# Two attention layers on one core: where the second layer's values, the projections and the next image's transposes stand in the order of work

## The chip, the core and the metric

The kernel runs on one core of a Trainium2 chip. The metric is device microseconds for one execution, the median of repeated runs; lower is better. Engines are named as in the profile: PE is TensorE (PEld its weight loads), DVE is VectorE, ACT ScalarE, POOL GpSimd, SP SyncE. Each has its own queue, and semaphores join them.

## The reference

Eight images of 32 x 32 positions (N = 1024 rows) and C = 256 channels, all float32, pass through two attention layers:

```python
# layer 0: four heads of width C
qkv = xf @ W_qkv                                  # b n (h, 3C)
atten = softmax((q @ k.T) * C ** -0.5)            # per head, over the keys
res = concat_h(atten @ v) @ W_out + b_out
x = res + xf
# layer 1: one head with keys of width 32
f, g, h = x @ Wf + bf, x @ Wg + bg, x @ Wh + bh
o = softmax(g @ f.T) @ h
y = gamma * o + x
```

## The kernel before

**Work and steps.** Weights are folded first (`fold_weights`: query with key weights, value with output weights), so that layer 0 is, for each head and each block of 512 queries: scores (`Layer0.scores`, L558), exponentials, a product of the probabilities with the image (`products`, L655), and a projection with the folded value weights (`project`, L676). All of these go by `seven` (L235), a seven-product scheme for 2 x 2 blocks of matrices: it has three tasks, `one`, `two` and `three`. Each puts matmuls on PE and then the reads of their banks on ACT and DVE. The operands of its seven products are sums of blocks, made by DVE: `query_sums` of q, `key_sums` of the image (L421, tile `xs`), `sums` of the probabilities (L593, tile `ss`, four pieces of 1024 columns), and the `ysums` of `project` (tile `yt`).

The list `steps` (L956) has one entry for each unit (a head, or layer 1 of the image before) and each of its two blocks. Images 1 to 6 run head 0, head 1, layer 1 of the image before, head 2, head 3; the last image has layer 1 of image 6 after its four heads, and layer 1 of image 7 follows behind all steps. In the text, "the third head" is head 2.

**The order.** PE, DVE and ACT carry out exactly the order in which tasks are called. In each step of the loop at L982, `put(tasks, *at)` notes a place between 0 and 10 for each task; at the end of the step the tasks are called in the order of these places, and of their `put` where places are equal. SP and POOL, which issue the DMAs, are ordered by the scheduler. A step scores its own block, makes sums and product tasks `one` and `two` of the step before (`one` at L984), and product task `three`, the reciprocal (`invert`, L637) and the projection of the step before that (`two`).

**Names that the change touches.**

- Layer 1's first step (`blk == 0`): `values` (L786) has five tasks. The first sets a column of ones on POOL; each of the other four has eight matmul passes (`pr_v_l`) and one DVE read into `v_l` (L794). Also here: `scores` of layer 1 (`ps_l`, L811), the product of head 1's second block (`psx_y`, `psy_y`, `psz_y`), the projection of its first block (`psx_o`, `psy_o`), and `turned1`, four DVE transposes (L394) of the image behind.
- Banks: `seven` takes three of the six `ps` banks for scores and products. For a projection (`two_banks`) it takes both `psm` banks, one for `x`, one for `y` and `z`. Values, too, take a `psm` bank each.
- `adds` (L697): DVE multiplies the projected tile `o` by the reciprocals `invb` (L699); POOL then adds `o` to `x1T` by an accumulating DMA (L702). The tile `o` has one buffer, so the next projection's first writes to `o` (ACT's copy of the `x` bank, L284, and DVE) wait until that DMA has landed.
- `invert` makes four reciprocals per row on DVE (L641); SP writes them to DRAM (`inv`, L646) and reads them back as a row for all partitions (`invb`, L648).
- The next image's transposed copy: `turn_rows` (L401) gives 8 `moves`, each with four SP DMAs (L386, `x0T`), and `turned`, four DVE transposes of 32 x 32 squares (L394). `key_sums` come from the result. They stand around the third head.
- Before the first step: matmuls of a zero tile (L947) while the first weights load, then transposes and products of weights (L312, L327, L365).

Of the kernel before, what the change touches and what calls it, by code (L numbers as in the profile page):

```python
# [20 lines left out]
def kernel(  # L21
# [89 lines left out]
    def tile_of(tag, shape, name):  # L111
        return pools[tag].tile(shape, F32, tag=tag, name=name)
# [4 lines left out]
    def load_x(b, parts=1):  # L117
        t = tile_of("rows", [P, NT, C], f"x_{b}")
        n = HT // parts
        for k in range(NBLK):  # L120
            for i in range(parts):
                nc.sync.dma_start(
                    t[:, k * HT + i * n : k * HT + (i + 1) * n, :].rearrange("p t c -> p (t c)"),
                    x_v[b][:, k, ts(i, n * C)],
                )
        rows[b] = t
# [78 lines left out]
    def sum_a(sums, a11, a12, a21, a22):  # L205
        tt = nc.vector.tensor_tensor
        s1, s2, s3, s4 = sums
        return [
            partial(tt, s1, a21, a22, ALU.add),
            partial(tt, s2, s1, a11, ALU.subtract),  # L210
            partial(tt, s3, a11, a21, ALU.subtract),
            partial(tt, s4, a12, s2, ALU.subtract),
        ]
# [11 lines left out]
    def a_operands(blocks, sums):  # L225
        a11, a12, a21, a22 = blocks
        s1, s2, s3, s4 = sums
        return dict(zip((1, 2, 3, 4, 5, 6, 7), (a11, a12, s4, a22, s1, s2, s3)))
# [172 lines left out]
    def turn_rows(b):  # L401


        def end():
            if b not in xT_of:
                xT_of[b] = tile_of("xT", [P, CC, N], f"x0T_{b}")
            return xT_of[b].rearrange("p c (n i) -> p c n i", i=P)

        return squares(end, lambda: rows[b].rearrange("p n (c i) -> p n c i", i=P), False)
# [11 lines left out]
    def key_sums(b):  # L421

        made = {}

        def piece(i):
            if i == 0:
                xT = xT_of[b]
                t = tile_of("v", [P, 4, HN], f"xs_{b}")
                sums = [t[:, k, :] for k in range(4)]
                blocks = [xT[:, c, ts(k, HN)] for k in range(2) for c in range(CC)]  # L430
                made["l"] = sum_a(sums, *blocks)
                xblocks[b] = a_operands(blocks, sums)
            made["l"][i]()

        return [partial(piece, i) for i in range(4)]

    def value_sums(b):

        made = {}

        def piece(i):
            if i == 0:
                r = rows[b]
                t = tile_of("xt", [P, 4, NT // 2, P], f"xt_{b}")
                blocks = [r[:, ts(j, NT // 2), ts(c, P)] for j in range(2) for c in range(CC)]
                sums = [t[:, k] for k in range(4)]
                made["l"] = sum_b(sums, *blocks)
                vblocks[b] = b_operands(blocks, sums)
            made["l"][i]()

        return [partial(piece, i) for i in range(4)]

    def residual(b):


        def piece(c):
            if c == 0:
                x1T_of[b] = tile_of("xT", [P, CC, N], f"x1T_{b}")
            nc.scalar.activation(
                x1T_of[b][:, c, :], xT_of[b][:, c, :], AF.Identity, bias=boutT_sb[:, c : c + 1]  # L460
            )

        return [partial(piece, c) for c in range(CC)]
# [479 lines left out]
    nc.vector.memset(idle, 0.0)  # L943
    ident = identity()
    pm = tile_of("psm", [P, NB], "pm_idle")
    for _ in range(5):
        nc.tensor.matmul(pm[:, :P], lhsT=idle, rhs=idle, start=True, stop=True)  # L947
    for h, tag in ((1, "rows"), (2, "v"), (3, "xT")):
        run(load_weights(h, tag))
# [6 lines left out]
    steps, adds = [], {}  # L956
# [16 lines left out]
    def is_l0(s):  # L973
        return s is not None and isinstance(s[0], Layer0)

    def step(k):
        return steps[k] if 0 <= k < len(steps) else None
# [4 lines left out]
    for i, (a, blk) in enumerate(steps):  # L982
        l0 = isinstance(a, Layer0)
        one, two, nxt = step(i - 1), step(i - 2), step(i + 1)  # L984
        places = []

        def put(tasks, *at):
            assert len(tasks) == len(at)
            places.extend(zip(at, range(len(places), len(places) + len(at)), tasks))

        if l0:
            put(a.scores(blk), 0, 2, 4, 6, 8, 10)
        else:
            tasks, _ = a.scores(blk)
            put(tasks, *((0.5, 2.4) if blk == 0 else (0.5, 2)))
        if is_l0(two):
            u, k = two
            put(u.products_of[k][2:], 1 if l0 else 0)
            if nxt is None:
                put([partial(u.invert_all, k)], 2.2)  # L1000
            put([partial(u.invert, k)], 3.4 if l0 else 2.7)
            ysums, tasks, adds[i] = u.project(k)
            put(ysums, *((1.1, 1.2, 1.3, 3.3) if l0 else (2.6, 2.7, 2.8, 3.1) if blk == 0 else
                         (1.1, 1.2, 1.3, 2.1)))
            put(tasks, *((3, 5.5, 7) if l0 else (5.2, 6, 7.2) if blk == 0 else
                         (3, 5, 7) if nxt else (2.1, 3.9, 4.1)))
            if nxt is None:
                put(adds[i], 5)
        if i - 1 in adds:
            put(adds[i - 1], 0.5 if l0 or blk == 1 else 2.3)  # L1010
        if is_l0(one):
            u, k = one
            sums, keys = u.sums(k)
            u.products_of[k] = u.products(k)
            put(sums, *((2.1, 3.2, 4.2, 5.6) if l0 else (0.8, 2.2, 3.5, 5.5)))
            put(keys, *((6.3, 6.6, 7.6, 8.7) if l0 else (6.3, 7.6, 8.3, 8.7)))
            put(u.products_of[k][:2], *((5, 9) if l0 else (4, 7)))
        elif one is not None:
            put(one[0].products(one[1]), *((3, 5, 7, 9) if l0 else (1, 4, 6, 8) if nxt else (1, 4, 7.2, 8.5)))
        if i == 0:  # L1020
            put(fold[0][2:] + fold[1], -2, -1, 0.5, 1.5, 2.5, 4.5, 6.5, 8.5)
            put(first_sums[:2], 8.4, 9.4)
        if i == 1:
            put(first_sums[2:], 1.4, 3.4)
            put(fold[2], 0.5, 2.6, 3.5, 5.5, 7.5)
            put([partial(nc.vector.tensor_scalar, bh_sb, bh_sb, gamma_sb, None, ALU.mult)], 8.5)

        if l0 and blk == 0:
            put(a.query_sums(1), 3.5, 4.3, 4.4, 5.3)
        if is_l0(nxt) and blk == NBLK - 1:  # L1030
            put(nxt[0].queries(), *((2.5, 4.5, 6.5) if not l0 else
                                    (1.5, 2.5, 4.5) if is_l0(two) else (0.5, 2.5, 5.5)))
            put(nxt[0].query_sums(0), *((6.7, 6.9, 7.3, 7.6) if not l0 else
                                        (5.4, 6.4, 7.2, 7.4) if is_l0(two) else (6.4, 7.2, 7.3, 7.4)))

        if l0 and a.h == 0 and blk == 1:
            put(residual(a.b), 5.3, 7.3)
        if l0 and a.h == 0 and blk == 1 and a.b > 0:
            put(value_sums(a.b), 1.4, 2.4, 3.4, 4.4)
        if l0 and a.h == 1 and blk == 0 and a.b + 1 < B:  # L1040
            load_x(a.b + 1)
        if is_l0(nxt) and nxt[0].h == 2 and nxt[1] == 0 and nxt[0].b + 1 < B:
            moves, turned = turn_rows(nxt[0].b + 1)
            put(moves[:4], 1, 3, 5, 7)
        if l0 and a.h == 2 and a.b + 1 < B:
            if blk == 0:
                put(moves[4:], 1, 3, 5, 7)
            else:
                put(turned, 0.7, 1.4, 2.4, 3.4)
                put(key_sums(a.b + 1), 5.7, 6.4, 7.4, 8.3)  # L1050

        if l0 and a.b > 0 and a.h == behind(a.b) - 1:
            if blk == 0:
                moves, turned1 = turn_back(a.b - 1)
                put(moves[:4], 3, 4.5, 6, 7.5)
            else:
                put(moves[4:], 4, 5.5, 7, 8.5)
                tasks, moves = nxt[0].queries_apart()
                put(tasks, 1.5)
                put(moves, 1.6, 1.7, 1.8, 1.9)  # L1060
        if not l0 and blk == 0:
            put(a.values(), 0.9, 1, 3, 5, 8)
            put(turned1, 2.5, 2.9, 4.2, 5.1)
        if nxt is None:
            fg = final.queries()
            moves, turned1 = turn_back(B - 1)
            put(moves, *[9.1 + 0.1 * k for k in range(8)])
        for _, _, t in sorted(places, key=lambda x: x[:2]):
            t()
# [90 lines left out]
    with tc.If(bad > 0), ExitStack() as general:  # L1160
# [7 lines left out]
        for b in range(B):  # L1168
# [3 lines left out]
            for h in range(HEADS):  # L1172
                a = General0(b, h, bout_sb)
# [4 lines left out]
            a = Layer1(b)  # L1178
# [37 lines left out]
```

## Time and profile before

| | |
|---|---|
| median of 3 runs | 2327.11 us (2326.35 to 2327.97) |
| profiled execution | 2329.28 us |
| its span, first to last instruction | 2327.5 us |
| granted TensorE clock, mean | 0.999 |
| DVE, ACT, POOL busy | 71%, 25%, 14% |
| `x1T<-o` accumulates (POOL DMA) | 64, 512 KB each, median 5.0 us to landing |
| `x0T<-x` moves (SP DMA) | 224, 32 KB each |

The span has eight images, some 286 us each, then the end of layer 1 for the last image. A matmul of 128 x 256 float32 is recorded as two passes, each with its weight load. In answers of the trace a line gives an instruction's start, its duration, engine, line, operation, what it writes and reads, shapes, the number merged into the line, and in brackets the idle time of its engine before it with what ended it. Matmul ends are modelled and overlap the next start.

### The profile page before, as it was taken

To read this page: it belongs to the slowest core of one execution; us is meant where nothing else is said; L and a number is where in the kernel's file an instruction comes from. 1 tells how busy PE (TensorE), PEld (TensorE's weight loads), DVE (VectorE), ACT (ScalarE), POOL (GpSimd) and SP (SyncE) were. 2 spreads that over 40 slices of the span, in tenths; PEclk is the share of its full clock that TensorE was granted. 3 is DMA by queue.
4 is the path that set the end of the run, shared out by engine and by line. 5 is a ranking of instruction groups with operands and counts; after the bars stand their busy time and mean duration, and the time that the engine had idled before them with its cause. 6 is when DMAs were issued, how large, how long until landed. Compare 5 with 4: busy or idle time off the path is not lost. (4 is left out here: it accounts for less than half of the span.)

```text
span 2327.5 us, 27263 instructions
## 1 busy us (share of the span) xinstructions
PE 2305.0 (99%) x10250; PEld 1892.2 (81%) x10250; DVE 1655.6 (71%) x2963; ACT 585.0 (25%) x1015; POOL 317.8 (14%) x199
## 2 busy tenths in 40 slices
PE   9999999999999999999999999999999999999999
PEld 7888887788877888778887888878888788888877
DVE  6778786477765777657776677766777567877755
ACT  2222222222221222212232122221222222222223
POOL 0111112011120111101121011210112101111210
PEclk9999999999999999999999999999999999999999
DMA  4211123301242012420133211342113311121231
GB/s 136 33 28 24 23 38 49 76 14 28 33 54 67 14 28 46 46 62 14 28 55 41 57 15 28 57 41 56 19 23 58 41 37 19 28 46 25 38 44 49
DMA packets 239740, 94.16 MB, mean 40 GB/s; under 512 B 204208, under 2 KB 208944, under 8 KB 239600
## 3 DMA queue, kind: packets, MB, share of 16 engines
q1 hardware_dynamic: 220400, 55.10, 12.2%
q0 software_dynamic: 19200, 37.23, 11.2%
q8 instruction: 83, 1.36, 0.5%
q14 instruction: 57, 0.47, 0.1%
HBM read 29.76 MB, written 8.65 MB: 17 GB/s over the span
## 5 line engine op out<-in xcount | busy, mean ns | idle before, releaser
L625 POOL PARTITION_ALL_REDUCE rb<-rs x64 | 206.6, 3228 | 1449.7 <-DVE rs L623 923.3
L255 PE MATMUL psx<-q,x0T 128*128 128x256 f32 x1024 | 263.5, 380 | 0.0
L575 ACT ACTIVATE p<-p 128x1024 f32<-128x1024 f32 x128 | 135.3, 1057 | 509.1 <-DVE p L272 509.1
L255 PE MATMUL psy<-qs,xs 128*128 128x256 f32 x1024 | 262.9, 379 | 0.0
L255 PE MATMUL psz<-q,xs 128*128 128x256 f32 x1024 | 262.8, 379 | 0.0
L255 PE MATMUL psx_y<-p,x 128*128 128x256 f32 x1024 | 241.9, 379 | 0.0
L255 PE MATMUL psy_y<-p,xt 128*128 128x256 f32 x1024 | 241.9, 379 | 0.0
L899 PE MATMUL pa_l<-v_l,s_l 128*128 128x257 f32 x1024 | 231.3, 381 | 0.0
L255 PEld LDWEIGHTS psx<-q,x0T 128*128 128x128 f32 x1024 | 193.8, 190 | 45.4 <-issue 20.7
L255 PEld LDWEIGHTS psx_y<-p,x 128*128 128x128 f32 x1024 | 194.6, 190 | 34.1 <-issue 8.6
L899 PEld LDWEIGHTS pa_l<-v_l,s_l 128*128 128x128 f32 x1024 | 194.0, 190 | 32.2 <-issue 5.3
L255 PEld LDWEIGHTS psy<-qs,xs 128*128 128x128 f32 x1024 | 194.4, 190 | 26.9 <-DVE q L272 0.4
L255 PEld LDWEIGHTS psy_y<-p,xt 128*128 128x128 f32 x1024 | 194.6, 190 | 26.5
L255 PEld LDWEIGHTS psz<-q,xs 128*128 128x128 f32 x1024 | 194.6, 190 | 26.4
L284 ACT ACTIVATE p<-psx 128x512 f32<-128x512 f32 x128 | 76.4, 597 | 359.5 <-PE psx L255 359.3
L272 DVE TENSOR_TENSOR u<-psy,e 128x512 f32<-128x512 f32 x128 | 88.1, 688 | 84.9 <-ACT e L278 73.4
L702 POOL DMA_DIRECT2D x1T<-o x64 | 78.0, 1219 | 431.1 <-DVE o L699 310.1
L255 PE MATMUL psy<-qs,x0T 128*128 128x256 f32 x512 | 132.3, 381 | 4.5 <-DVE v L272 4.4
L272 DVE TENSOR_TENSOR v<-psy,e 128x512 f32<-128x512 f32 x128 | 88.3, 690 | 56.6 <-PE psy L255 55.3
L255 PE MATMUL psy_y<-ss,xt 128*128 128x256 f32 x512 | 121.4, 380 | 3.7 <-DVE ss L612 3.7
L255 PE MATMUL psz_y<-ss,xt 128*128 128x256 f32 x512 | 121.0, 379 | 0.0
L255 PE MATMUL psz_y<-ss,x 128*128 128x256 f32 x512 | 120.9, 379 | 0.0
(141 smaller groups left out, 3415.9 us busy)
## 6 DMA issues: line engine op xcount, KB each, us to landing
x1T<-o POOLq DMA_DIRECT2D x64, 512.0 KB, 5.0
invb<-inv SPq DMA_DIRECT2D x63, 256.0 KB
x<-x1T SPq DMA_DIRECT2D x256, 32.0 KB
out_dram<-x SPq DMA_DIRECT2D x15, 512.0 KB
x<-in_x_dram SPq DMA_DIRECT2D x14, 512.0 KB
x0T<-x SPq DMA_DIRECT2D x224, 32.0 KB
fg<-v_l POOLq DMA_DIRECT2D x56, 64.0 KB, 2.1
w<-in_L_conv_W_qkv_dram SPq DMA_DIRECT2D x4, 512.0 KB
```

The costliest lines, as they stand in the source:

```text
L255: nc.tensor.matmul(banks[k][:, ts(i, w)], lhsT=lhsT, rhs=rhs, start=first and n == 0, stop=True, skip_group_check=True,)
L272: nc.vector.tensor_tensor(dst, shaped(banks[k]), shaped(other), ALU.add)
L284: copy(outs["11"](), shaped(banks["x"]))
L575: exp(both, both)
L625: nc.gpsimd.partition_all_reduce(t, r.rearrange("p e i -> p (e i)"), P, bass_isa.ReduceOp.add)
L702: nc.gpsimd.dma_start(x1T_of[self.b][:, :, ts(blk, NB)], o, accum_op=ALU.add)
L899: nc.tensor.matmul(pm[:, : C + 1], lhsT=p[:, j, ts(ti, P)], rhs=v[:, j, : C + 1], start=(j == 0), stop=(j == NT - 1),)
```

## The change

It moves tasks within or between steps and adds three zero matmuls. No computation that enters the result changes.

```diff
@@ before the first step
-    for _ in range(5):
+    for _ in range(8):
         nc.tensor.matmul(pm[:, :P], lhsT=idle, rhs=idle, start=True, stop=True)
@@ projections (tasks of the step before last)
-            put(ysums, *((1.1, 1.2, 1.3, 3.3) if l0 else (2.6, 2.7, 2.8, 3.1) if blk == 0 else
-                         (1.1, 1.2, 1.3, 2.1)))
-            put(tasks, *((3, 5.5, 7) if l0 else (5.2, 6, 7.2) if blk == 0 else
-                         (3, 5, 7) if nxt else (2.1, 3.9, 4.1)))
+            put(ysums, *((1.1, 1.2, 1.3, 3.3) if l0 else (1.1, 1.2, 1.3, 2.5) if blk == 0 else
+                         (0.6, 0.7, 0.8, 0.9)))
+            put(tasks, *((3, 5.5, 7) if l0 else (4.5, 6, 7.2) if blk == 0 else
+                         (3, 5, 7) if nxt else (1.9, 3.1, 4.1)))
             if nxt is None:
-                put(adds[i], 5)
+                put(adds[i], 4.2)
@@ products (of the step before)
-            put(u.products_of[k][:2], *((5, 9) if l0 else (4, 7)))
+            put(u.products_of[k][:2], *((5, 9) if l0 else (4, 5)))
         elif one is not None:
-            put(one[0].products(one[1]), *((3, 5, 7, 9) if l0 else (1, 4, 6, 8) if nxt else (1, 4, 7.2, 8.5)))
+            put(one[0].products(one[1]), *((3, 5, 7, 9) if l0 else (1, 4, 6, 8) if nxt else (1, 3, 4, 8.5)))
@@ the next image's moves, transposes and key sums
             moves, turned = turn_rows(nxt[0].b + 1)
-            put(moves[:4], 1, 3, 5, 7)
+            put(moves[:4], 1, 2.5, 4, 5.5)
         if l0 and a.h == 2 and a.b + 1 < B:
             if blk == 0:
-                put(moves[4:], 1, 3, 5, 7)
+                put(moves[4:], 0.5, 1.5, 2.5, 3.5)
+                put(turned, 6.4, 7.4, 8.4, 9.4)
             else:
-                put(turned, 0.7, 1.4, 2.4, 3.4)
-                put(key_sums(a.b + 1), 5.7, 6.4, 7.4, 8.3)
+                put(key_sums(a.b + 1), 0.5, 0.6, 6.4, 7.4)
@@ layer 1's values, first step
-            put(a.values(), 0.9, 1, 3, 5, 8)
+            put(a.values(), 0.9, 1, 2.3, 3, 6.5)
```

So in layer 1's first step the four value tasks stand ahead of the product except for the last, and the product's two tasks stand between those of the projection. In layer 1's second step only `ysums` move, and the first four moves. In the last step the projection's tasks stand behind row products. The four transposes go from the third head's second step to its first, and two of the key sums to the front of the second.

## The prediction

> **What bounds the kernel now.** I read the busy times first, then TensorE's waits, then the windows of the four steps that the change touches, then the timelines around the waits.
>
> ```profile
> PE 2305.0 (99%) x10250; PEld 1892.2 (81%) x10250; DVE 1655.6 (71%) x2963; ACT 585.0 (25%) x1015; POOL 317.8 (14%) x199
> ```
>
> TensorE bounds the kernel: the matmuls stay as they are, so only its gaps can be won. Its waits, summed:
>
> ```profile
> PE psy L255 <- DVE v L272: 4.4, 8, 0.8
> PE psy_y L255 <- DVE ss L612: 3.7, 6, 0.6
> PE psy_o L255 <- DVE v_l L794: 2.9, 7, 0.4
> PE pwq L312 <- DMA w<-in_L_conv_W_qkv_dram: 1.3, 1, 1.3
> PE psy_o L255 <- DVE u_o L272: 1.1, 7, 0.2
> ```
>
> Each recurs once an image, VectorE ends it, and the whole list is 17 us: 0.7% is all that can be had. A wait costs a bit more than it shows, since a matmul's modelled end reaches past the start of the next. I count in starts: a 256-column pass follows the one before after 0.2165 us (eight take 1.73), and after a wait the second pass comes 0.10 late (679.64 to 680.18 is 0.54 for two).
>
> One image's four steps (Layer 1 first step, second step; third head first, second):
>
> ```profile
> 662.28:687.94 25.66, 25.09 (x120) 19.68 (x119) 17.68 (x31) 7.20 (x14) 1.44 (x2) 1.00 0.49 42
> 691.40:716.80 25.40, 25.40 (x109) 18.13 (x109) 12.49 (x27) 5.94 (x12) 3.15 (x2) 1.00 0.33 48
> 716.82:742.77 25.95, 25.95 (x121) 22.80 (x120) 11.92 (x24) 3.94 (x6) 1.19 (x1) 1.00 0.28 63
> 742.77:771.17 28.40, 27.24 (x111) 20.72 (x110) 22.90 (x37) 7.21 (x12) 0.05 (x1) 1.00 0.16 56
> ```
>
> After the duration: PE, PEld, DVE busy. VectorE is 46% busy in the third head's first step and 81% in its second; PE has gaps only in the first and last row. The last row's, from the timeline:
>
> ```profile
> 752.34 0.70 DVE L394 STREAM_TRANSPOSE x0T<-x0T 128x512 f32<-128x512 f32 x1
> 754.26 1.22 DVE L612 TENSOR_TENSOR ss<-ss,p 128x1024 f32<-128x1024 f32 x1
> 755.62 1.97 PE L255 MATMUL psy_y<-ss,xt 128*128 128x256 f32 x8 [0.62 <-DVE ss L612]
> 767.40 0.68 DVE L433 TENSOR_TENSOR xs<-x0T 128x512 f32<-128x512 f32 x1
> 768.60 0.68 DVE L272 TENSOR_TENSOR v<-psy,e 128x512 f32<-128x512 f32 x1
> 769.34 0.92 PE L255 MATMUL psy<-qs,x0T 128*128 128x256 f32 x3 [0.55 <-DVE v L272]
> ```
>
> A transpose and a key sum of the next image stand ahead of what TensorE waits for. And the first row's:
>
> ```profile
> 672.56 1.26 POOL L702 DMA_DIRECT2D x1T<-o  x1 [10.10 <-ACT s_l L820]
> 672.99 0.36 SPq L646 DMA_DIRECT2D inv<-inverse  x1
> 679.64 0.70 PE L255 MATMUL psy_o<-yt,wo 128*128 128x256 f32 x2 [0.41 <-DVE v_l L794]
> 681.36 0.70 PE L255 MATMUL psy_o<-yt,wo 128*128 128x256 f32 x2 [0.15 <-DVE u_o L272]
> 682.87 0.37 ACT L284 COPY o<-psx_o 128x256 f32<-128x256 f32 x1 [3.23 <-DVE v_o L272]
> ```
>
> **What the Trainium skill says.** "PSUM — Partial Sum Buffer", section "Engine vs sequencer instructions": ScalarE and VectorE queues are strict FIFO and matmuls start in program order. The trace agrees: the sum at 754.26 stands behind a transpose it doesn't need. "DMA: Bandwidth & Descriptors", section "Queues, rings and completion order": a DMA's semaphore increment lands only after every earlier write of that DMA engine, across its queues. It fits: the accumulate at L702 lands in a median 5.0 us, but in 9.7 to 12.9 in Layer 1's seven first steps, where an `inv` DMA is issued 0.44 us behind it; `invb`, which waits for `inv`, is issued at 681.98, and `o`'s next writer (682.87) had waited for the accumulate. "TensorE: Matmul & The Clock Gate", Part 1: the clock is halved until about 3.4 us of sustained activity; here the first eight `pwqk` passes take 3.19 us, the same eight later 1.89.
>
> **Part 1, third head (six images, and image 0 in part).** Removed from the second step: four transposes, each 0.62 of queue time (752.34 to 752.96). The first two key sums come to the place of the first two transposes, where VectorE has 0.62 us to spare before `v` at 749.87: 1.40 against 1.30, hidden. Without the transpose at 752.34 the sum starts at 753.63 and ends at 754.85; TensorE wants it at 753.11 + 1.73 = 754.84. The loss of 755.62 - 754.84 = 0.78, plus 0.07 between the passes after it, becomes about 0.04. Then VectorE runs without a gap from `q` at 760.21 to `v` at 768.60: 8.39, in it three key sums of 0.60; two remain ahead of `v`, so 7.79. `q` follows TensorE, now 0.75 earlier: 759.46 + 7.79 = 767.25, `v` ends 767.93, wanted at 768.63 - 0.75 = 767.88. The loss of 0.71 + 0.10 becomes 0.19. Gain 1.67 - 0.23 = 1.44 an image, six times: 8.6. Image 0 has only the second wait, 0.24 + 0.10: 0.3.
> Added to the first step: four transposes in VectorE's gaps (3.57 before 736.06, 1.04 before 737.78, 2.05 before 741.25): hidden. They need the 32 `x0T` moves: SP ends issuing them at 722.8, the hardware DMA queue has no packets of data left after 726, and the first transpose would start at 732.5: 6 us or more of cover. If it went, VectorE's queue would stop and each microsecond past some 4 reach TensorE. Moves placed earlier change little: SP already issued far ahead, and is held by the wait for `inv` (709.9 to 716.4). Whether `invb` then comes sooner or later by a move or two (0.65 each) is unknown: 0; TensorE lost 0.93 there once, at 437.
>
> **Part 2, Layer 1's first step (seven images).** New PE order from 662.28 = 0: three (3.46), scores, values 1 (4.62), values 2 (6.45), scores (8.27), values 3 (9.35), product one (11.18), projection one (16.37), product two (17.67), projection two (21.13), values 4 (21.99), projection three. Both old waits go (0.58 + 0.32, with 0.10 each after: 1.10): the banks of values 2 and 3 are read out by 13.8, and projection two comes 3.5 us after `u_o`.
> New waits. Projection one takes both `psm` banks, so values 4 needs ScalarE's copy of `psx_o` (L284) done: 21.13, 0.64 from a `psx_o` to its reader (678.63 to 679.26), the copy's 0.37 and 0.05 to TensorE make 22.19, a loss of 0.20 + 0.10. VectorE stands behind `v_y` (product two) until 21.33; then `v_y` (0.46), `y` (0.40), a transpose (0.63), the last sum (1.13, as 681.22 to 682.35), and only then `v_o`, 23.95 to 24.37. Projection three, ready at 24.02, waits to 24.42: 0.40 + 0.10. Step 24.56 + 0.3 + 0.5 = 25.39 against 25.66: gain 0.27.
> But that copy also waits for the accumulate's landing (one `o` buffer). The product with `invb` (L699) now stands behind three `ysums` and moves from 8.45 to 9.55; the accumulate follows at 11.4 (1.83 later, as before) and `inv`, behind values 2, a `ysums` and a transpose, at 12.47. Old landings came 9.3 to 12.4 after `inv`: so 21.7 to 24.9. Up to 22.2 it costs nothing; beyond, the step ends at landing + 3.16. Lower bound: the gap to `inv` grows from 0.44 to 1.09 and the accumulate slips through in 5 us: 7 x 0.27 and the 1.1 that two old steps (at 1543 and 2237) lost to late landings, -2.9. Upper: all at 24.9, where the step ends at 28.06 against a mean of 25.81: +15.7. Three old landings in seven were late; I take two (24.3, ending at 27.4, +1.7 each) and five not: +2.0.
>
> **Part 3, the last step.** Projection one comes after the first row product, two after the second: waits of 0.56, 0.40 and the pieces after go, 1.5. The last accumulate starts 1.8 later, so 32 `x<-x1T` moves do too and the final transposes stop VectorE some 3 us, of which about 0.7 reaches TensorE: -0.8 (-1.5 to +0.5). Second-step `ysums` 0.5 earlier: no wait there, 0.
>
> **Part 4, the start.** Three more zero matmuls are six passes of 0.21: done at 4.63, before the weights at 4.81, so free. If they fill the activity window, the clock doubles earlier than about 10.9: transposes and `pwqk` lose up to 2.2. Bounds 0 and -2.2; -1.5.
>
> **Sum**: -8.6 - 0.3 + 2.0 - 0.8 - 1.5 = -9.2. The profiled execution took 2329.28 (span 2327.5 and 1.8 around it): 2320.1; the median shown, 2327.11, is 2.2 lower: 2318.
>
> **Rivals.**
> - All covers hold: the accumulate lands early, start and end give all: -8.9 - 2.9 - 1.5 - 2.2 - 1.0 (the stall at 437) = -16.5: 2310.6. For it: the longer gap to `inv`; against: the rule on increments.
> - Layer 1 gives it back: most landings near 24, +10: 2326. For it: three of seven old landings were over 12.
> - Slower, the same queue grown into the bound: values 4 behind the copy behind the accumulate. Price: 1 us an image for each microsecond past 22.2. The old seven average 25.81, so a mean landing of 24.25 (7 x 1.6) eats all of the 11.2 won elsewhere, and from 24.9 it is slower beyond 0.2%; at 26.0, 7 x 3.35 = 23.5, 2339. Against it: a landing at 26 would be 13.5 after `inv`, and the longest seen is 12.4.
>
> **How the numbers follow.** Main 0.52 (2312 to 2323), all covers 0.20, given back 0.18, slower 0.10. 0.2% is 4.65 us, about what a measurement here tells from nothing: faster below 2322.5. From main 0.50, covers 0.20 and given back 0.05: faster 0.75; slower 0.10; same 0.15. Range 2309 to 2327: it leaves out the slower case and the edges.
>
> **What would show it.** Right: no `psy_y <- ss` wait, `psy <- v` under 0.15 each, new waits of `pr_v_l` on ScalarE's `o` and of `psy_o` on `v_o` in Layer 1's first step, none in the third head's first; `pwqk` at nearly 1.9. Wrong: waits at the third head's first step, or Layer 1 first steps over 27 in most images.

## The result and the profile after

The changed kernel takes 2317.34 us, the median of six runs (2316.86 to 2318.83), against 2327.2 of the kernel before beside it: 9.9 us less, a ratio of 0.9958 with a 95% interval of 0.9946 to 0.9971. Its profiled execution took 2317.21, with a span of 2315.4. That of before took 2329.28, 2.1 above its median; some 2 us of it are single stalls (at 437, 1543 and 2237 us). That the median lacks them is likely but not shown, since one execution alone has a trace. So the two spans are 12.1 apart and the medians 9.9.

The busy line of the page, and the largest of TensorE's waits (total, times, longest):

```profile
PE 2302.4 (99%) x10256; PEld 1892.5 (82%) x10256; DVE 1661.6 (72%) x2963; ACT 585.5 (25%) x1015; POOL 317.9 (14%) x199
```

```profile
PE psy_o L255 <- DVE o L272: 4.2, 7, 0.6
PE pm_idle L947 <- DVE col L134: 1.1, 1, 1.1
PE pwvo L327 <- ACT x0T L368: 0.8, 1, 0.8
PE px L365 <- DVE wqk L175: 0.3, 1, 0.3
PE psy L255 <- DVE v L272: 0.3, 1, 0.3
```

The four waits that recurred once an image (on `v`, `ss`, `v_l`, `u_o`: 12.1 us together) are gone from the list, but for one on `v` at 31.57, in image 0. One new wait stands in their place, seven times: the projection's `psy_o` on VectorE's `o`. The four steps of one image:

```profile
658.20:683.92 25.72, 25.09 (x120) 19.68 (x118) 16.76 (x29) 7.20 (x14) 1.43 (x2) 1.00 0.26 42
687.40:712.80 25.40, 25.40 (x109) 18.13 (x109) 13.32 (x27) 5.94 (x12) 3.87 (x2) 1.00 0.32 46
712.80:738.70 25.90, 25.90 (x121) 22.77 (x120) 13.94 (x28) 3.94 (x6) 1.19 (x1) 1.00 0.28 60
738.76:766.00 27.24, 27.22 (x111) 20.73 (x110) 21.43 (x35) 7.21 (x12) 0.65 (x1) 1.00 0.17 59
```

After the duration come PE, PEld and DVE busy. Layer 1's first step (the first row) gained nothing: 25.72 against 25.66. The third head's second step gained 1.16, and VectorE carries 2.0 us more in its first step (13.94 for 11.92) and 1.5 less in its second (21.43 for 22.90).

### The profile page after: what moved, and what is told of

Same layout as the page of the kernel before. It is cut to its first block, busy times and chain, and to the rows that moved or that the text cites. A ratio compares the mean times of both kernels' runs of the same rounds, so it can differ in the third digit from the quotient of the medians.

```text
span 2315.4 us, 27268 instructions
## 1 busy us (share of the span) xinstructions
PE 2302.4 (99%) x10256; PEld 1892.5 (82%) x10256; DVE 1661.6 (72%) x2963; ACT 585.5 (25%) x1015; POOL 317.9 (14%) x199
## 3 DMA queue, kind: packets, MB, share of 16 engines
q8 instruction: 83, 1.36, 0.4%
## 4 chain that ended last, share of the span: by engine, by line
PE 98%; DVE 1%; issue 0%; ACT 0%; DVEq 0%
PE psy_y L255 14%; PE psy L255 14%; PE pa_l L899 10%; PE psx L255 10%; PE psz L255 10%; PE psx_y L255 10%; PE psz_y L255 10%; PE psy_o L255 6%; PE psy_q L255 4%; PE psx_q L255 2%; PE psz_q L255 2%; PE psx_o L255 2%; PE pr_v_l L493 2%; PE ps_l L811 1%; PE pm_fg L766 1%; DVE ss L612 0%
## 5 line engine op out<-in xcount | busy, mean ns | idle before, releaser
L702 POOL DMA_DIRECT2D x1T<-o x64 | 78.0, 1219 | 424.2 <-DVE o L699 301.8
```

The costliest lines, as they stand in the source:

```text
L702: nc.gpsimd.dma_start(x1T_of[self.b][:, :, ts(blk, NB)], o, accum_op=ALU.add)
```

## The experiments

The runs stand in three groups, each with the kernel before beside it. Its medians differ (2327.9, 2328.7 and 2329.0), so each run is compared with the median of its own group.

| run | us | less before of its group | ratio, 95% interval |
|---|---|---|---|
| third head's part alone | 2319.86 | -8.1 | 0.9966 (0.9954 to 0.9978) |
| eight zero matmuls alone | 2326.54 | -1.4 | 0.9995 (0.9987 to 1.0003) |
| Layer 1's first step alone | 2327.21 | -0.7 | 0.9997 (0.9989 to 1.0006) |
| last step alone | 2327.42 | -0.5 | 0.9997 (0.9989 to 1.0006) |
| changed, sum ahead | 2312.14 | -16.6 | 0.9931 (0.9918 to 0.9945) |
| changed, keys behind | 2319.70 | -9.0 | 0.9962 (0.9948 to 0.9975) |
| both | 2314.41 | -14.3 | 0.9941 (0.9927 to 0.9954) |
| both, keys close | 2310.07 | -18.9 | 0.9922 (0.9908 to 0.9935) |
| changed, gap short | 2320.51 | -8.2 | 0.9970 (0.9958 to 0.9982) |
| before, gap long | 2327.69 | -1.3 | 0.9996 (0.9987 to 1.0004) |

### The four parts, each alone on the kernel before

The third head's part is the moves, `turned` and `key_sums` lines of the change; the zero matmuls are `range(8)`; Layer 1's first step is the `blk == 0` places of `ysums` and `tasks`, `(4, 5)` for the product, and `values`; the last step is the rest.

> The kernel before with the third head's part alone: moves, transposes in the first step, two key sums at the front of the second. Theory (the changed trace read by its parts): 1.15 us for each of six images and 0.3 in image 0, about -7.2, so 2320.0; the waits of psy_y on ss and of psy on v shrink, none comes in the third head's first step. Rival 1, the prediction's own size (1.44 an image): -8.9, 2318.3. Rival 2, that part of the gain only appears because Layer 1's part calmed the DMA queues (the late inv at 437 gone): here -7 or less, and single stalls behind a late invb stay.

> The kernel before with eight zero matmuls instead of five and nothing else. Theory: the filled stretch before the weights makes the clock double near 5.9 us instead of 10.9, the first transposes and the first eight pwqk passes get short (3.19 to about 2.0), and everything after starts 1.6 us earlier: 2325.6. Rival: the earlier clock is an effect of how the start happened to fall in one execution; then pwqk takes 3.2 us again and the time stays at 2327.2.

> The kernel before with the part of Layer 1's first step alone: values ahead of the product, product tasks at 4 and 5, projection tasks at 4.5, 6 and 7.2, ysums earlier. Theory: the two old waits go (-1.1 a step), the new waits cost 0.3 at the fourth values and 0.87 at the third projection task, so each undisturbed step stays at 25.7; what is gained is what late landings of the accumulate and late inv rows cost in single steps: 0 to -1.5, 2326.5; the accumulates in these steps land in 6 to 9 us instead of 9.7 to 12.9. Rival (the prediction): the third projection waits 0.40 on v_o, the step takes 25.39 and two landings come late: +2.

> The kernel before with the last step's part alone (and the ysums of the other second steps of Layer 1 half a place earlier, where no wait is): Theory from the changed trace: -1.4 to -1.7, 2325.7, as the waits before projections one and two go and the later transposes stop nothing that PE needs. Rival (the prediction's term): -0.8, with 0.7 us of the final transposes reaching TensorE.

Measured: -8.1, -1.4, -0.7 and -0.5, in sum -10.7, against -9.9 for the whole. Only the first is outside what a measurement tells from nothing. It is most of the change's gain; in its trace each of the six second steps is 1.15 us shorter than before (28.40), as in the changed kernel:

```profile
740.08:767.33 27.25, 27.23 (x112) 20.77 (x110) 21.43 (x35) 7.21 (x12) 0.66 (x1) 1.00 0.16 59
```

No stall of over 0.11 is left in the third head's first steps, at 437 either. That settles rival 2: the part needs no help from Layer 1's. The -8.1 lies between the theory and the prediction's size, and one median can't choose between them; the trace does: six times 1.15, and 0.35 in image 0, are 7.2.

In the run of Layer 1's first step alone the waits are those of the changed kernel:

```profile
PE psy_o L255 <- DVE o L272: 3.6, 6, 0.6
PE pr_v_l L493 <- ACT o L284: 0.9, 1, 0.9
```

Seven steps, and seven long waits: six on `o`, and one, in the last first step, on ScalarE's copy, held by an accumulate that landed after 10.97 us. So the two old waits (1.10 a step) were exchanged for two new ones (1.16).

The last step's part shows in its trace 1.4 us less in that step, and 0.4 more in the stretch after it, of which a 0.27 stall at 2294 is one piece. In the changed kernel that stretch is 0.3 shorter than before. What sets it is open.

### What the new wait in Layer 1's first step waits for

VectorE and TensorE of the changed kernel there:

```profile
679.50 0.42 DVE L272 TENSOR_TENSOR v_y<-psy_y,e_y 128x256 f32<-128x256 f32 x1 [2.96 <-PE psy_y L255]
679.96 0.42 DVE L272 TENSOR_TENSOR y<-psz_y,v_y 128x256 f32<-128x256 f32 x1
680.30 0.70 DVE L394 STREAM_TRANSPOSE x<-x 128x512 f32<-128x512 f32 x1
680.92 1.18 DVE L612 TENSOR_TENSOR ss<-p,ss 128x1024 f32<-128x1024 f32 x1
682.03 0.41 DVE L272 TENSOR_TENSOR v_o<-psy_o,e_o 128x256 f32<-128x256 f32 x1
682.47 0.42 DVE L272 TENSOR_TENSOR o<-psy_o,v_o 128x256 f32<-128x256 f32 x1
```

```profile
680.35 1.99 PE L493 MATMUL pr_v_l<-wh_sb,x1T 128*128 128x256 f32 x8
682.95 0.70 PE L255 MATMUL psy_o<-yt,wvo 128*128 128x256 f32 x2 [0.60 <-DVE o L272]
```

The third projection task writes `psy_o` from 682.95, right after the second read, `o`, ends at 682.89, and not after `v_o` (682.44). In all seven steps it starts 0.05 to 0.06 after `o` and 0.51 after `v_o`. `y` and `z` share a `psm` bank (`two_banks`), and `o` reads `z`. The transpose and the sum ahead of `v_o` don't belong to this wait, and VectorE is idle before `v_y` for 2.96. So they were moved there, on the changed kernel:

```diff
-            put(sums, *((2.1, 3.2, 4.2, 5.6) if l0 else (0.8, 2.2, 3.5, 5.5)))
+            put(sums, *((2.1, 3.2, 4.2, 5.6) if l0 else (0.8, 2.2, 3.5, 5.5 if blk else 4.6)))
-            put(turned1, 2.5, 2.9, 4.2, 5.1)
+            put(turned1, 2.5, 2.9, 4.2, 4.7)
```

> The changed kernel with two VectorE tasks of Layer 1's first step moved: the last sum of probabilities and the last transpose stand ahead of the product's second read (places 4.6 and 4.7) instead of behind it. Theory: the third projection task waits for the second read of the y and z bank, which stands behind v_y, y, a transpose and a sum; with the last two gone it ends at about 681.2 (in the times of the changed trace) while TensorE comes at 682.1, so the 0.77 and the 0.10 after it go in all seven steps, 6.1 in all: 2311.2; the fourth values still wait 0.19 for ScalarE's copy. Rival (the prediction's reading, v_o alone counts): the same step, since both reads come early; told apart only by the size: 0.40 and 0.10 a step, -3.5, 2313.8. Second rival: the sum or the transpose, now earlier, stops something else on VectorE (u_o at the next bank) and the gain is under 2.

Measured: 2312.14; in the trace each of the seven steps is 0.87 shorter, 6.1 in all, and the wait has left the list. One of the steps, and what the list now begins with:

```profile
656.99:681.84 24.85, 24.82 (x119) 19.79 (x118) 17.11 (x29) 7.20 (x14) 1.43 (x2) 1.00 0.19 33
```

```profile
PE pm_idle L947 <- DVE col L134: 1.1, 1, 1.1
PE pwvo L327 <- ACT x0T L368: 0.8, 1, 0.8
```

The size is that of the whole wait (0.77 and 0.10). The edit brought both reads forward, so it doesn't tell them apart; that the wait was for the second one is read from the times above.

### The rest of the third head's waits

Two small waits are left in each second step: 0.18 and 0.07 at `psy_y`, 0.16 and 0.10 at `psy`. Both show in the changed kernel only as late starts:

```profile
749.04 0.69 DVE L272 TENSOR_TENSOR q<-psz_q,v_q 128x512 f32<-128x512 f32 x1
749.64 1.22 DVE L612 TENSOR_TENSOR ss<-ss,p 128x1024 f32<-128x1024 f32 x1
...
759.77 0.68 DVE L433 TENSOR_TENSOR xs<-x0T 128x512 f32<-128x512 f32 x1
...
762.24 0.69 DVE L433 TENSOR_TENSOR xs<-x0T,xs 128x512 f32<-128x512 f32 x1
762.84 0.69 DVE L619 TENSOR_TENSOR rs<-rs,ss 128x512 f32<-128x512 f32 x1
763.44 0.68 DVE L272 TENSOR_TENSOR v<-psy,e 128x512 f32<-128x512 f32 x1
```

```profile
749.09 1.89 PE L255 MATMUL psx_y<-p,x 128*128 128x256 f32 x8
751.00 1.97 PE L255 MATMUL psy_y<-ss,xt 128*128 128x256 f32 x8
...
762.29 1.89 PE L255 MATMUL psy_y<-p,xt 128*128 128x256 f32 x8
764.18 1.13 PE L255 MATMUL psy<-qs,x0T 128*128 128x256 f32 x4
```

`psy_y` could start at 749.09 + 1.73 = 750.82 and starts at 751.00; `psy` at 762.29 + 1.73 = 764.02 and starts at 764.18. Ahead of the one stands the queries' read `q`, ahead of the other two key sums (`xs`). The edit, on the changed kernel:

```diff
-            put(sums, *((2.1, 3.2, 4.2, 5.6) if l0 else (0.8, 2.2, 3.5, 5.5)))
+            put(sums, *((2.1, 2.2 if a.h == 2 and blk else 3.2, 4.2, 5.6) if l0 else (0.8, 2.2, 3.5, 5.5)))
-                put(key_sums(a.b + 1), 0.5, 0.6, 6.4, 7.4)
+                put(key_sums(a.b + 1), 0.5, 0.6, 8.2, 9.3)
```

> The changed kernel with three VectorE tasks of the third head's second step moved: the last two key sums behind the read v (places 8.2 and 9.3), and the second sum of probabilities ahead of the queries' second read (2.2 for 3.2). Theory: the rest of both waits goes (0.18 and 0.07 at psy_y, 0.16 and 0.10 at psy), 0.52 for six images, -3.1: 2314.2. Rival: the queries' read, now 1.1 us later, keeps TensorE from their bank or the following p and u reads late, and the gain is taken back (2317 or more).

> Both edits together on the changed kernel. Theory: the two lie in different steps and add up: -9.2 against the changed kernel, 2308.1. Rival: an earlier third projection brings the next adds and accumulate 0.9 us earlier against the other DMAs, and late landings or late inv rows take back 1 to 3.

Measured: 2319.70 and 2314.41. The theory failed. The rival had the late `p` right, but not its cause. In the trace the two waits are gone (0.52), and a new one costs 0.81 an image (0.71, and 0.10 after it), also 0.33 in image 0: `psz` on VectorE's `p`. From GpSimd's, VectorE's and TensorE's timeline of the first of the two runs:

```profile
764.67 3.23 POOL L625 PARTITION_ALL_REDUCE rb<-rs  x1 [43.53 <-issue]
```

```profile
763.48 0.68 DVE L433 TENSOR_TENSOR xs<-x0T 128x512 f32<-128x512 f32 x1
764.08 0.42 DVE L623 TENSOR_TENSOR rs<-rs 128x256 f32<-128x256 f32 x1
...
765.21 2.24 DVE L433 TENSOR_TENSOR xs<-x0T,xs 128x512 f32<-128x512 f32 x1
767.37 0.68 DVE L272 TENSOR_TENSOR p<-psy,e 128x512 f32<-128x512 f32 x1
767.97 0.68 DVE L272 TENSOR_TENSOR p<-psz,u 128x512 f32<-128x512 f32 x1
```

```profile
768.10 1.13 PE L255 MATMUL psz<-q,xs 128*128 128x256 f32 x4 [0.55 <-DVE p L272]
```

The last key sum takes 2.24 instead of 0.69. It lies beside GpSimd's all-reduce (764.67 to 767.90), and both its inputs are in SBUF; the reads of PSUM at 764.42 and 764.87, beside the same all-reduce, keep their 0.42. The Trainium skill, "SBUF — State Buffer", section "Who interferes with whom", says just this: a VectorE instruction with two SBUF inputs contends with a GpSimd instruction that reads SBUF, and the one issued second blocks.

The traces of before and after already had a case of it. In Layer 1's second step VectorE multiplies `o` by `invb`, both in SBUF; alone that takes 1.22 us, here 1.49 before and 2.22 after:

```profile
690.12 3.22 POOL L625 PARTITION_ALL_REDUCE rb<-rs  x1 [16.30 <-issue]
691.93 1.49 DVE L699 TENSOR_TENSOR o<-o,invb 128x1024 f32<-128x1024 f32 x1
```

```profile
686.83 3.22 POOL L625 PARTITION_ALL_REDUCE rb<-rs  x1 [15.84 <-issue]
687.91 2.22 DVE L699 TENSOR_TENSOR o<-o,invb 128x1024 f32<-128x1024 f32 x1
```

Take from each end the time that the instruction needs alone: 691.93 + 1.49 - 1.22 is 2.08 after the all-reduce began, 687.91 + 2.22 - 1.22 is 2.08, and for the key sum 765.21 + 2.24 - 0.69 is 2.09. So it is in every one of the 112 cases in the fourteen profiles, whether VectorE's instruction was issued 0.5, 0.8, 1.1 or 1.8 us after the all-reduce: it is held until 2.08 to 2.09 us into it and then takes its own time. That agrees with the page, but for the end: it goes on while the all-reduce is still recorded as running for 1.1 us more.

If so, the key sum has only to stand ahead of the reduction (L623) that releases the all-reduce:

```diff
-                put(key_sums(a.b + 1), 0.5, 0.6, 8.2, 9.3)
+                put(key_sums(a.b + 1), 0.5, 0.6, 8.2, 8.3)
```

> As the run with both edits, but the last key sum at 8.3 instead of 9.3, so that it stands ahead of the last reduction of the sums (L623), whose end starts GpSimd's all-reduce, and not beside that all-reduce, where it took 2.24 us instead of 0.69. Theory: the key sum takes 0.69 again, the wait of psz on p that cost 0.73 an image goes, both edits' gains stand: 0.87 x 7 + 0.52 x 6 = 9.2 below the changed kernel, 2308.1 (2309 against the before kernel of that call, 2328.7). Rival: p and u reads stand 0.6 us later in any case, and the wait at psz stays (0.3 or more an image), so 2311 to 2313.

Measured: 2310.07, 18.9 below before, the fastest kernel here. The key sum is short again, and neither of the old waits nor the new one is left. The second step of the same image, and the key sum in it:

```profile
737.61:764.34 26.73, 26.73 (x112) 20.90 (x111) 21.27 (x34) 7.21 (x12) 0.40 (x1) 1.00 0.17 60
```

```profile
762.75 0.68 DVE L433 TENSOR_TENSOR xs<-x0T,xs 128x512 f32<-128x512 f32 x1
763.35 0.42 DVE L623 TENSOR_TENSOR rs<-rs 128x256 f32<-128x256 f32 x1
```

Each of the six second steps is 0.52 shorter than in the changed kernel, and six of the seven first steps are 0.87 shorter, as expected. Its profiled execution gives back 2.1 of the 9.2: the start took 0.6 longer, a late `invb` cost 0.5 at 435 us, and in the last first step an accumulate landed after 11.1 us, which cost the 0.87 and 0.1 more. So 2310 against an expected 2309.

### What decides when the accumulate lands

In Layer 1's seven first steps the accumulate (L702) landed in 9.7 to 12.9 us before and in 6.3 to 9.2 after. The change has put 1.10 us between it and the `inv` DMA, for 0.44. To test the gap alone, it was made short on the changed kernel, as below, and long on the kernel before, with 2.85 in the place of 2.45:

```diff
-            put([partial(u.invert, k)], 3.4 if l0 else 2.7)
+            put([partial(u.invert, k)], 3.4 if l0 else 2.7 if blk else 2.45)
```

> The changed kernel with the reciprocals of Layer 1's first step right behind the second values (place 2.45 for 2.7), so that the inv DMA is issued about 0.3 us after the accumulate instead of 1.10. Theory: the gap decides: the accumulates in the seven first steps land in 9.2 to 12.9 us again, a landing beyond 10.2 holds ScalarE's copy of the x bank, and three or so steps end 1 to 2 us later, so +3 to +5: 2321. Rival: the landings came down because the accumulate stands elsewhere among the x moves; then they stay at 6.3 to 9.2 and the time at 2317.3.

> The kernel before with the reciprocals of Layer 1's first step two ysums later (place 2.85 for 2.7), so that the inv DMA is issued some 1.3 us after the accumulate instead of 0.44; nothing else is changed. Theory: the gap alone decides the landing: the accumulates of the seven first steps land in 6.1 to 11 us instead of 9.2 to 12.9, and the two steps that a late landing lengthened (0.19 and 0.74) come back: -0.9. Rival: the landing hangs on the other DMAs of the place (x moves, the next image's loads); then it stays at 9.2 to 12.9.

Short (a gap of 0.17): landings of 9.5 to 12.1. In the trace three steps pay 1.09, 0.72 and 0.62, 2.4 in all, somewhat less than the 3 to 5 expected; the median lies 8.2 below its own before, where the changed kernel lies 9.9 below. One of the three steps, in the order POOL, SP, ACT, PE:

```profile
954.94 1.26 POOL L702 DMA_DIRECT2D x1T<-o  x1 [11.36 <-ACT s_l L820]
```

```profile
955.11 0.36 SPq L646 DMA_DIRECT2D inv<-inverse  x1
```

```profile
967.10 0.37 ACT L284 COPY o<-psx_o 128x256 f32<-128x256 f32 x1 [3.74 <-DMA x1T<-o]
```

```profile
967.52 1.99 PE L493 MATMUL pr_v_l<-wh_sb,x1T 128*128 128x256 f32 x8 [1.99 <-ACT o L284]
```

The landing (12.06 after 954.94) releases ScalarE's copy, and the copy the fourth values: 1.99 lost. The third projection, which follows, then doesn't wait, so the step is 1.1 longer, not 2.

Long (a gap of 1.36): six of the seven landings come down to 5.1 to 7.0. The seventh, in the last image, took 13.2, and its cause is open. So the gap decides, except in the last image: there six of the eight profiles with 1.10 have a landing of 11.0 to 11.8 too. But part of the delay only moves: with a gap of 0.44 `invb` is issued 8.7 to 11.2 us after `inv` in these steps, with 1.36 after 10.8 to 13.4, and the stall on a late `invb` near 437 us is 1.6 there, for 0.9 before. The time, -1.3 with an interval across zero, says nothing.

The packet records show that two different delays go into a landing. Of the accumulate's 256 data packets, 47 to 52 take over 0.6 us before and 45 to 52 with the short gap, and the last packet ends 9.1 to 12.6 us after the issue: the data itself is late. In the changed kernel and with the long gap no packet takes that long, and the last one ends after 4.8 to 5.3 us, or 6.2 in the last image of the long gap. What is late there is the landing's signal: 1.5 to 4.0 us behind the last packet in the changed kernel, and 7.0 in that last image. The prediction's rule on increments would fit this second delay, though no run here tests it; it doesn't describe the first, since `inv` is issued behind the accumulate and it is the accumulate's own data that comes late.

### How many zero matmuls

> The changed kernel with seven zero matmuls, so that TensorE is idle for some 0.6 us before the first weights instead of 0.2. Theory (a share of a window must be filled): the clock still doubles, at or shortly after 5.9 us, first eight pwqk passes near 2.0 us. Rival (any gap restarts the count): pwqk takes 3.2 us again and everything after starts 1.6 us later.

> The changed kernel with six zero matmuls, idle for some 1.0 us before the first weights. Theory (share of a window): one more gap of 0.4 may be too much; pwqk between 2.0 and 3.2 us. Rival: 3.2 us as with five, since the window from 1.06 us was filled only with eight.

Matmuls of the zero tile and the first weights, with seven of them and with six:

```profile
1.06 3.35 PE L947 MATMUL pm_idle<-idle 128*128 128x128 f32 x14 [1.06 <-DVE col L134]
5.29 0.63 PE L312 MATMUL pwq<-ident,w 128*128 128x128 f32 x4 [0.88 <-DMA w<-in_L_conv_W_qkv_dram]
```

```profile
1.06 2.93 PE L947 MATMUL pm_idle<-idle 128*128 128x128 f32 x12 [1.06 <-DVE col L134]
5.18 1.09 PE L312 MATMUL pwq<-ident,w 128*128 128x128 f32 x4 [1.19 <-DMA w<-in_L_conv_W_qkv_dram]
```

With seven the first weights already go in short passes (0.63 for four against 1.09), with six `pwqk` takes 2.78. Each is one execution (2318.22 and 2319.00 us), and the moment of change moves between executions: in the run with the keys behind, which has eight, it came at 4.17, while the zero matmuls still ran. So with seven it may have come before the gap of 0.88, and whether a gap restarts the count stays open. Two numbers of matmuls don't give a threshold either.

## Why the prediction was right

The forecast was 2318; 2317.34 was measured. The third head's and the start's mechanisms were right and carry the gain. That the sum, -9.2, came so near to the -9.9 of the medians is in part luck: the third head gained 1.7 less than forecast and Layer 1's first step cost 1.5 less; the latter is itself the sum of two errors, +2.3 and -3.9.

- **Third head, -8.6.** Right in mechanism and nearly in size: 1.15 an image instead of 1.44, so 6.9 for six. The mis-sized term is what remains of the two losses, taken as 0.04 and 0.19 and measured as 0.26 and 0.26. At `psy_y` the sum came only 0.03 later than counted; left out were the 0.14 from the sum's end to TensorE's start (750.86 to 751.00; before, 755.48 to 755.62) and the 0.08 lost between the passes after it. At `psy` VectorE took 7.85 from `q` to `v` for the 7.79 counted, with two key sums still ahead of `v`. The run with both edits and the keys close shows that this rest was to be had. The new first step is free, as predicted.
- **Layer 1's first step, -0.27 in an undisturbed step.** The fourth values' wait was exact: 0.20 and 0.10 predicted, 0.19 and 0.10 measured. The step that failed is "Projection three, ready at 24.02, waits to 24.42: 0.40". It took `v_o` for the end of the wait, where it is the second read of the shared bank, 0.42 later: 0.77. So the step gains nothing (+0.06), and moving the sum and the transpose brought the whole 0.87 back. The Trainium skill, "PSUM — Partial Sum Buffer", section "PSUM bank collisions raise a hardware error", says to guard by bank and not by address; read beside `two_banks` it would have given the right read, and the seven starts 0.05 to 0.06 after `o` agree. The trace shows the wait, not whether it comes from such a rule or from how the program tracks its tiles.
- **The landings, two late ones of +1.7.** None was late in the profiled execution: 6.3 to 9.2 after the issue, when the copy has 10.2. (In six of the seven other profiles with this gap the last of the seven lands at 11.0 to 11.8, and that step is 0 to 1.0 longer than the other six; so one late landing or none, not two.) The prediction saw the longer gap and priced it as the lower bound, "the accumulate slips through"; it took the old spread for the likelier. The gap runs show that the gap took the old spread away, though the landings still come 1.3 to 4.2 us later than the 5 of the bound. This error of -3.9 outweighs the one at the third projection, +2.3 in the seven steps.
- **The start, -1.5.** Right: TensorE's first query product starts at 14.55 for 16.17, 1.6 earlier, and 1.4 earlier in the trace of that part alone (its median, -1.4, has an interval across zero). Before, then after:

```profile
8.48 3.19 PE L327 MATMUL pwqk<-wqT 128*128 128x256 f32 x8
```

```profile
8.05 1.99 PE L327 MATMUL pwqk<-wqT 128*128 128x256 f32 x8 [0.24 <-ACT x0T L368]
```

- **The last step, -0.8.** -1.4 in the trace of the step, near its lower bound: the 0.7 that the final transposes were to cost TensorE didn't come. The medians can't tell it from nothing.
- **Rivals.** "Slower, the same queue" has its mechanism shown in the short-gap run, at a price of 0.6 to 1.1 us a late step, but in the changed kernel's trace no landing comes to that point. "All covers hold" had the landings right. It was counted from the median, though the main sum had already taken 2.2 off for the stalls that this rival takes off once more (1.1 and 1.0): 2312.7, not 2310.6.
- **Two slips of reading.** In the list of waits before, the line on `pwq` isn't one that recurs: a DMA ends it, once. And 24.56 + 0.3 + 0.5 is 25.36, not 25.39. Neither changes the outcome.

## What to carry to other kernels

Where two outputs share a bank, a matmul that writes one may wait for the read of the other, as in all seven steps here: find the last read of the bank, then look what stands ahead of it in its queue without need. An edit that moves work off a late read must look at the engine next door as well, since a sum that takes 0.69 us in one place took 2.24 in another. And a DMA's landing time can hang on what is issued within a microsecond after it: before pricing a landing, measure the distance to the next issue.

## What the hardware showed that was not expected

- A VectorE instruction with two SBUF operands, issued behind the start of GpSimd's all-reduce, is held until 2.08 to 2.09 us into it and then takes its own time (2.24 us for 0.69, 1.49 or 2.22 for 1.22), in all 112 cases; reads of PSUM beside it kept their time, and so did the one transpose beside it, with a single SBUF operand (0.70).
- The accumulate's landing against the gap to the `inv` DMA behind it: 9.5 to 12.1 us at 0.17, 9.7 to 12.9 at 0.44, 6.3 to 9.2 at 1.10 in the changed kernel (5.7 to 11.8 over all profiles with that gap), 5.1 to 7.0 at 1.36 (six of seven). Up to 0.44 the data packets are late, from 1.10 on only the signal behind them.
- The moment at which TensorE's passes become short moves between runs of the same start: from 4.2 to 7.5 us in the seven profiles with eight zero matmuls, from 8.9 to 11.1 in the five with five. That fits a free-running window, as the Trainium skill has it ("TensorE: Matmul & The Clock Gate", Part 1). The durations are all that the trace shows of it: the granted clock of the profile stands at 1.00 from 1 to 12 us in both. So the part's gain varies from run to run; over these profiles the first query product starts 1.3 us earlier in the mean (14.5 for 15.9).
